# Two residual additions as identity products, and an order of its own for the first attention

## The chip, the cores and the metric

The kernel runs on one core of one Trainium2 chip. Times are microseconds (us) on the device for one launch. A core has five engines that run side by side, each with its own instruction queue: PE (TensorE, matrix products[...]), DVE (VectorE), ACT (ScalarE), POOL (GpSimd) and SP (which here only issues transfers). Each engine takes its instructions in the order in which they stand in its queue. The kernel before was timed three times: 9422.48, 9424.92 and 9425.63 us.

## What is computed

Two layers, each with a residual, on x of 8 images, 256 channels, 48 x 48 = 2304 positions. Layer 0 is an attention over positions that keeps the 16 most similar ones. Layer 1 is a stack of two selective scans (Mamba) over the 2304 positions.

```python
def _L0_conv_ref(x, W, bias):
    tokens = x.reshape(b, c, n).transpose(0, 2, 1)
    feat_pos = tokens @ W.T + bias
    feat, pos = feat_pos[:, :, :c], feat_pos[:, :, c:]
    pos = pos / jnp.maximum(norm, 1e-12)
    sim = jnp.einsum('bnc,bmc->bnm', pos, pos)
    topksim, topkid = jax.lax.top_k(sim, K)              # K = 16
    attn = jax.nn.softmax(topksim, axis=-1)
    out = jnp.einsum('bnk,bnkc->bnc', attn, topkfeat)
...
def step(h, inp):                                        # one of 2304 steps, 512 channels x 16 states
    dt_t, B_t, C_t, x_t = inp
    dA = jnp.exp(dt_t[:, :, None] * A)
    h = h * dA + dt_t[:, :, None] * B_t[:, None, :] * x_t[:, :, None]
    y = jnp.einsum('bds,bs->bd', h, C_t)
...
# --- layer 0 (conv_preact) ---
x = x + _L0_conv_ref(_gn(x), L0_conv_W, L0_conv_bias)
# --- layer 1 (conv_preact) ---
x = x + _L1_conv_ref(_gn(x), ...)                        # two Mamba layers, each after a layer norm
```

The change concerns the two lines `x = x + ...`.

## The kernel before

**The two parts of the program.** The attention of image 0 runs alone at the start (`layer0(..., alone=True)`, lines 591 to 617). After that the scans of images 0 to 7 run one after another, and beside the scans of image b the attention of image b + 1 is carried out, a little at each step (class `Ahead`). The last image has no attention beside it.

**Units and half steps.** An image's positions are cut into 6 chunks of 384. A *unit* is one chunk of one of the two Mamba layers, so there are 12 units an image and 96 in all, in an order in which the second layer runs two chunks behind the first. A unit has 16 *steps*. A step handles 32 of the 512 channels with all 16 states, laid out as 32 channels x 4 groups of states on the 128 partitions and 4 states along the free dimension. A step falls into two *half steps* of two states each. The main loop runs over half steps m; a unit has 32 of them.

**What a half step does.** POOL makes the forcing term of a whole step, `bx` (L907, 128x1536), two steps ahead. ACT makes the two decays of a half step (L928), one half step ahead, into one of two PSUM banks. DVE runs the scan (L943). The product of the states with C is then taken either by DVE (L945, for one half step, letter V in the string `SHARE`) or by POOL (L971, for one or both half steps of the step before, letter G). PE sums the states into `y` (L989), and with that frees the `bx` buffer, of which there are 8. `SHARE` has three strings of 32 letters: the first for the units 1 to 9 of an image, beside which the top-k of the next image runs, the second for the other units, the third for the last image.

**Tables.** All the other work of a unit (loads, layer norm, projections, taps, softplus, silu, gates, `out_proj`, `leave`) is placed by hand in tables of pairs (half step, function). Negative half steps lie in the unit before, those above 31 in the unit after. `between` and its kin come ahead of the half step's scan in the program, `behind` and its kin after it. The tables with `_spare` are for the units without top-k, those with `_last` for the last image.

**The attention.** Its 18 blocks of 128 positions take 16 half steps each, two blocks a unit. The list `within` says at which half step of its block each part stands: similarities on PE and their copies on ACT (`similar`, `keep_similar`, for blocks two ahead), the top-k on DVE (`top`, four instructions of 2.54 us), the turned weights (`turn`, `weights`), the weighted sum (`weigh`), then `average` (22), `turn_back` and `finish` (both 24). The same list serves for the attention of image 0, where no scan runs beside it and only the order of the instructions counts. Before its blocks each attention has a preparation of some 50 half steps (projections, norms), which starts at half step `EARLY` of the image ahead. The blocks begin at the next half step that fits into a raster of 16.

**The two residual additions.** `finish` (L551, DVE) adds the transposed attention in PSUM to the rows of x in SBUF. The rows come by a transfer that `average` issues on SP for every third block, into one of three buffers of the tag "x". `leave` (L1024, DVE) adds, for the second Mamba layer, the product in PSUM, a bias and the rows of x1 in SBUF, and a transfer takes the sum out. For the first Mamba layer `leave` is a copy on ACT (L1020). PSUM tiles of PE come from four banks used in turn (tag "mm"). A bank is free when its reader, here the DVE addition, is done.

Of the kernel before, what the change touches and what calls it, by code (L numbers as in the profile page):

```python
# [11 lines left out]
AF = mybir.ActivationFunctionType  # L12
ALU = mybir.AluOpType
# [3 lines left out]
P = 128  # L17
# [9 lines left out]
def tile_conv_preact(  # L27
# [18 lines left out]
    nc = tc.nc  # L46
# [5 lines left out]
    CB = C // P  # L52
    DB = DI // P
# [3 lines left out]
    TB = T // P  # L57
# [14 lines left out]
    FOLDED = (2, 3,)  # L72
    EARLY = -21


    SHARE = (
        "GGVGGGVGGGVVGVGGGGGVGGGVGGGGGVVG",
        "GVGGGVVVGGVVGGGGVGGVGGVVVGVVGVGV",
# [182 lines left out]
    def layer0(b, left, pool, ps0, alone):  # L261
# [229 lines left out]
        def invert(t):  # L491
            nc.vector.reciprocal(blocks[t]["den"], blocks[t]["den"])

        def others(t, i):
# [36 lines left out]
        def average(t):  # L531
            row = blocks[t]
            row["o"] = pool.tile([P, C], F32, tag="o", name=f"o_{b}_{t}", bufs=more)
            nc.scalar.activation(row["o"], row["po"], AF.Identity, scale=row["den"])
            if t % TB == 0:
                tag, bufs = ("xr", 2) if alone else ("x", 3)
                rows[t // TB] = load_chunk(pool, x[b], t // TB, tag, f"xr_{b}_{t}", bufs)

        def turn_back(t):
            row = blocks[t]  # L540
            row["pr"] = mm0(C, f"pr_{b}_{t}")
            for cb in range(CB):
                nc.tensor.transpose(
                    row["pr"][:, cb * P : (cb + 1) * P], row["o"][:, cb * P : (cb + 1) * P], ident
                )

        def finish(t):
            row = blocks[t]
            c, j = divmod(t, TB)
            xr = rows[c][:, :, j * P : (j + 1) * P]  # L550
            nc.vector.tensor_add(xr, xr, row["pr"].rearrange("p (k t) -> p k t", k=CB))  # L551
            if j + 1 == TB:
                xr = rows.pop(c)
                for cb in range(CB):
                    nc.vector.bn_stats(st1[:, cb, c, :], xr[:, cb, :])
                nc.sync.dma_start(x1[:, c * T : (c + 1) * T].rearrange("(k p) t -> p k t", p=P), xr)
            row.clear()
# [5 lines left out]
            (16, weigh, 0), (1, top, 1), (-9, similar, 0), (-7, similar, 1), (-7, similar, 2), (22, average),  # L563
            (-6, similar, 3), (-7, keep_similar, 1), (-3, keep_similar, 3), (-1, top, 0),
            (-3, keep_similar, 4), (15, turn, 1), (10, others, 4), (5, others, 0), (3, top, 2), (6, add_top),
            (12, invert), (5, others, 2), (17, turn, 2), (20, turn, 3), (24, finish), (15, weights, 1),
            (18, turn, 4), (18, weights, 2), (21, weigh, 3), (7, others, 1), (19, weights, 4), (21, weigh, 4),
        ]
        begin = min(part for part, *_ in within)
        parts = {}  # L570
# [433 lines left out]
    def out_proj(unit, cb):  # L1004
        pw = unit["pw"][cb] = mm(T, f"pw_{unit['u']}_{cb}")
        for k in range(DB):
            nc.tensor.matmul(  # L1007
                pw, unit["ow"][:, k, cb * P : (cb + 1) * P], unit["z"][k],
                start=(k == 0), stop=(k == DB - 1),
            )  # L1010

    def leave(unit, cb):
# [9 lines left out]
        else:  # L1022
            res = unit["res"]
            nc.vector.scalar_tensor_tensor(  # L1024
                res[:, cb, :], unit["pw"][cb], b_feat[:, cb : cb + 1], res[:, cb, :], ALU.add, ALU.add
            )
# [25 lines left out]
        (-3, load_rep, "dt", 1), (-29, load_in, 2), (5, in_proj, 7), (-20, tap, 0), (-15, taps, 1),  # L1052
        (-2, load_rep, "dtx", 3), (38, leave, 1), (22, load_rep, "dtx", 15), (-8, load_in, 4), (-37, mean),
        (-19, taps, 0), (5, load_d, 1), (-19, in_proj, 1), (-10, load_bc, 0), (-30, root_end),
        (-9, times_x, 0), (29, gate, 2),
    ]
    between_spare = [
        (25, sum_states, 2), (-34, variance), (-21, in_proj, 0), (38, out_proj, 0), (-15, taps, 2),
        (-35, square), (39, leave, 0), (23, load_rep, "dt", 14), (5, load_rep, "dt", 5),
# [8 lines left out]
        (7, load_rep, "dt", 6), (17, load_rep, "dt", 12), (-6, load_rep, "dtx", 1), (-14, load_in, 7),  # L1068
        (37, gate, 3), (-31, root), (9, load_rep, "dt", 7), (5, load_d, 1), (-24, load_in, 3),
        (17, load_rep, "dt", 11), (14, load_rep, "dtx", 11), (-13, x_proj), (-17, load_in, 6), (-3, load_d, 0),  # L1070
# [8 lines left out]
        (-2, load_rep, "dtx", 3), (8, copy_z, 1), (22, load_rep, "dtx", 15), (-16, load_in, 4), (-38, mean),  # L1079
        (-22, normal), (-37, center), (-21, in_proj, 1), (-12, load_bc, 0), (-30, root_end), (-9, times_x, 0),  # L1080
        (-25, load_in, 1), (-28, scale),
# [9 lines left out]
        (-17, tap, 1), (21, load_rep, "dt", 13), (-20, tap, 0), (-10, step_size, 1), (-5, load_rep, "dt", 0),  # L1091
        (9, copy_z, 2), (-18, in_proj, 2), (2, load_rep, "dtx", 5), (10, sum_states, 0),
        (13, load_rep, "dt", 9), (33, gate, 2), (-2, in_proj, 4), (9, silu_z), (7, load_rep, "dt", 6),
# [125 lines left out]
```

## Time and profile before

| what | value |
|---|---|
| median of three runs | 9424.92 us |
| the profiled execution, own time | 9422.82 us |
| its span in the profile | 9421.1 us |
| granted TensorE clock, mean | 0.898 |
| L551, the additions of the attention, DVE | 144 of 407 ns, 58.6 us |
| L1024, the additions of the scan part, DVE | 96 of 606 ns, 56.4 us |
| L907, forcing terms, POOL | 1536 of 3462 ns, 5307.1 us |
| L971, products with C, POOL | 1317 of 2455 ns, 3233.3 us |
| L943, scans, DVE | 3072 of about 1.75 us, 5327.1 us |
| L928, decays, ACT | 6144 of 585 ns, 3592.8 us |
| L378, copy 128x256 from PSUM, ACT | 144 of 364 ns |
| L792, Identity with bias, 128x384 from PSUM, ACT | 24 of 567 ns |

How to read it: a line of groups gives the busy time of one instruction of the source, how often it ran and the mean time of one. The recorded times of one engine overlap a little from one instruction to the next, so the distance between starts is some 0.1 us less than the duration (a scan that lasts 1.75 us is followed by the next one after 1.67). A line of waits names the engine and line that waited, what released it, the sum in us, how often, and the longest. In a timeline the columns are start, duration, engine, line, operation, and in brackets the idle time before it with what ended it. The first scan starts at 468 us; POOL and DVE are busy 8782 and 8598 of the 8953 us from there to the end.

### The profile page before, as it was taken

The page shows a single profiled execution, that of the slowest core. Times are in us where ns is not written, and L with a number is a line of the kernel's source. Part 1 is how long each engine was busy: PE and PEld are TensorE (multiplying, and loading weights), DVE is VectorE, ACT ScalarE, POOL GpSimd, SP SyncE. Part 2 cuts the span into 40 slices and gives each one's busy share as a digit, 9 for nine tenths or more (in the row PEclk, how much of TensorE's full clock was granted, in tenths as well). Part 3 has the DMA queues.
Part 4 walks back from the last instruction along what each step waited for, and adds up shares of the span by engine and source line. Part 5 has one row for each costly group of instructions (what it writes and reads, how often), then busy time and mean ns, then how long its engine had stood idle before and what let it go on. Part 6 is the DMA issues. An engine that isn't in the chain of part 4 may idle for free. (4 is left out here: it accounts for less than half of the span.)

```text
span 9421.1 us, 120485 instructions
## 1 busy us (share of the span) xinstructions
PE 7867.0 (84%) x37049; PEld 4423.6 (47%) x37049; DVE 8867.3 (94%) x7543; ACT 7307.1 (78%) x16242; POOL 8867.9 (94%) x3605
## 2 busy tenths in 40 slices
PE   8888987888878898798878988788887888877676
PEld 6644544455544554455444545445554455433332
DVE  6599999999989999899999999999999999989999
ACT  4578877788778877787878787778877788777776
POOL 2199999999999999999999999999999999999999
PEclk9989998899989998899988999889998899988877
DMA  4134444444444444444444434443444344444443
GB/s 128 50 123 136 134 137 152 129 136 137 136 151 129 133 140 131 151 131 139 131 144 138 140 128 140 145 138 127 138 134 157 122 141 132 138 153 145 149 147 126
DMA packets 1029829, 1275.91 MB, mean 135 GB/s; under 512 B 106529, under 2 KB 998945, under 8 KB 1028417
## 3 DMA queue, kind: packets, MB, share of 16 engines
q1 hardware_dynamic: 1028640, 1268.21, 42.0%
q8 instruction: 296, 4.85, 0.2%
q14 instruction: 349, 2.85, 0.1%
q10 hardware_dynamic: 544, 0.00, 0.0%
HBM read 1050.77 MB, written 217.06 MB: 135 GB/s over the span
## 5 line engine op out<-in xcount | busy, mean ns | idle before, releaser
L907 POOL TENSOR_TENSOR bx<-BC,dtxr 128x1536 f32<-128x1536 f32 x1536 | 5307.1, 3462 | 33.0 <-PE y L989 30.4
L928 ACT ACTIVATE da<-dtr,A_sb 128x385 f32<-128x385 f32 x6144 | 3592.8, 585 | 928.3 <-DVE bx L943 601.8
L943 DVE TENSOR_TENSOR_SCAN bx<-da,bx 128x770 f32<-128x770 f32 x1986 | 3423.7, 1746 | 85.1 <-ACT da L928 78.7
L971 POOL TENSOR_TENSOR bx<-bx,BC 128x1536 f32<-128x1536 f32 (+1 forms) x1317 | 3233.3, 2455 | 103.7 <-DVE bx L943 91.6
L943 DVE TENSOR_TENSOR_SCAN da<-da,bx 128x770 f32<-128x770 f32 x1086 | 1903.4, 1753 | 125.5 <-ACT da L928 123.1
L527 PE MATMUL po<-feat,aT 128*128 128x256 f32 x5184 | 1378.8, 415 | 236.6 <-ACT dt L842 107.3
L698 PE MATMUL pe<-vn,inw 128*128 128x384 f32 (+1 forms) x2976 | 1175.7, 524 | 216.0 <-ACT vn L775 100.6
L527 PEld LDWEIGHTS po<-feat,aT 128*128 128x128 f32 x5184 | 1022.0, 205 | 633.9 <-ACT aT L516 167.4
L456 PE MATMUL psim<-pos 128*128 128x512 f32 x2520 | 1203.2, 619 | 130.6 <-DVE xr L551 85.4
L989 PE MATMUL y<-bx,sel 128*32 128x384 f32 x12288 | 1221.6, 527 | 72.7 <-POOL bx L971 72.4
L945 DVE TENSOR_TENSOR bx<-da,BC 128x768 f32<-128x768 f32 x1086 | 1040.6, 958 | 37.4
L698 PEld LDWEIGHTS pe<-vn,inw 128*128 128x128 f32 x2976 | 567.6, 201 | 648.0 <-ACT vn L775 125.1
L456 PEld LDWEIGHTS psim<-pos 128*128 128x128 f32 x2520 | 504.4, 209 | 709.8 <-issue 385.3
L989 PEld LDWEIGHTS y<-bx,sel 128*32 128x32 f32 x12288 | 400.5, 117 | 866.6 <-issue 683.2
L803 DVE SCALAR_TENSOR_TENSOR xc<-pe,cw,xc 128x384 f32<-128x384 f32 x1080 | 655.4, 612 | 33.2 <-ACT xc L794 7.8
L516 ACT ACTIVATE aT<-pt 128x512 f32<-128x512 f32 (+1 forms) x720 | 387.7, 547 | 330.9 <-PE pt L508 328.6
L1007 PE MATMUL pw<-z,ow 128*128 128x384 f32 x1536 | 551.0, 505 | 57.5 <-ACT aT L516 38.5
L507 PE MATMUL pt<-ident,sim 128*128 128x128 f32 x2592 | 540.1, 289 | 13.4 <-DVE v L762 5.6
L986 PE MATMUL y<-xc,dmat 128*128 128x384 f32 x768 | 380.7, 581 | 157.7 <-DMA dmat<-diag 43.7
L499 ACT ACTIVATE rest<-left,three 128x512 bf16<-128x512 f32 (+1 forms) x720 | 453.5, 669 | 64.6 <-DVE left L484 64.6
L508 PE MATMUL pt<-minus,rest 128*128 128x128 bf16 x2592 | 496.1, 225 | 3.0 <-ACT rest L499 3.0
L959 ACT COPY h_st<-da 128x2 f32<-128x2 f32 x884 | 138.5, 157 | 419.9 <-DVE bx L945 409.2
(160 smaller groups left out, 9933.9 us busy)
## 6 DMA issues: line engine op xcount, KB each, us to landing
dtxr<-dtx_d SPq DMA_DIRECT2D x1536, 192.0 KB, 2.9
dtr<-dt_d SPq DMA_DIRECT2D x1536, 192.0 KB, 2.8
BC<-bc_d SPq DMA_DIRECT2D x192, 768.0 KB, 5.6
inw<-in_in_wT_dram SPq DMA_DIRECT2D x744, 128.0 KB, 2.5
dtx_d<-dtx SPq DMA_DIRECT2D x384, 192.0 KB, 1.9
dt_d<-dt SPq DMA_DIRECT2D x384, 192.0 KB, 2.0
ow<-in_out_wT_dram SPq DMA_DIRECT2D x96, 512.0 KB, 4.5
dmat<-diag SPq DMA_DIRECT2D x384, 64.0 KB, 2.7
```

Source lines behind the costliest of these rows:

```text
L456: nc.tensor.matmul(pm, pos[:, k, t * P : (t + 1) * P], pos[:, k, c0 : c0 + w], start=(k == 0), stop=(k == CB - 1),)
L507: nc.tensor.transpose(pt[:, q], row["sim"][:, r], ident)
L527: nc.tensor.matmul(row["po"], aT[:, m % PT, :], feat[:, m, :], start=(m == 0), stop=(m == NB - 1))
L698: nc.tensor.matmul(pe, w[:, k], unit["vn"][:, k, lo:], start=(k == 0), stop=(k == CB - 1))
L803: nc.vector.scalar_tensor_tensor(unit["xc"][e], unit["pe"][e][:, k : k + T], cw[:, unit["d"], e, k : k + 1], unit["xc"][e], ALU.mult, ALU.add,
L907: nc.gpsimd.tensor_tensor(bx[:, :, 1:], unit["BC"][0], unit["dtxr"][i].unsqueeze(1).to_broadcast([P, Q, T]), ALU.mult,)
L928: nc.scalar.activation(da[:, s * (1 + T) : (s + 1) * (1 + T)], unit["dtr"][i], AF.Exp, scale=A_sb[:, unit["d"], i, p * HQ + s : p * HQ + s ...
L943: nc.vector.tensor_tensor_scan(h, da, g, 0.0, ALU.mult, ALU.add)
L945: nc.vector.tensor_tensor(bx[:, :, 0:T], da.rearrange("p (q t) -> p q t", q=HQ)[:, :, 1:], unit["BC"][1][:, qs], ALU.mult,)
L971: nc.gpsimd.tensor_tensor(g[:, :, 0:T], g[:, :, 1:], unit["BC"][1][:, qs], ALU.mult)
L989: nc.tensor.matmul(y[j * G : (j + 1) * G, :], sel, unit["bx"][k * J + j][:, q, 0:T], start=False, stop=True, skip_group_check=True,)
L1007: nc.tensor.matmul(pw, unit["ow"][:, k, cb * P : (cb + 1) * P], unit["z"][k], start=(k == 0), stop=(k == DB - 1),)
```

## The change

1. `turn_back` gets, after each of its two transposes, a product of the identity with 128 columns of the rows of x, accumulated onto the same PSUM columns. `finish` becomes a copy from PSUM to SBUF on ACT.
2. `out_proj` gets, for the second Mamba layer, a fifth product, of the identity with the rows of x1, accumulated onto the same bank. `leave` becomes an Identity with bias on ACT.
3. The load of the rows of x moves from `average` (half step 22 of the block) to `invert` (12).
4. The first attention gets a list of its own, `first_order`. In `within` one entry moves by one half step.
5. The first string of `SHARE` has its letters at half steps 13 and 14 exchanged. The preparation of the next image starts at -24 instead of -21.
6. Five entries of the tables move: the load of the fourth dtx two half steps earlier (`behind`), `variance` two later and `root` one earlier (`between_spare`), `root_end` one earlier (`behind_spare`), and one `in_proj` three earlier (`between_last`).

```diff
-    EARLY = -21
+    EARLY = -24
...
-        "GGVGGGVGGGVVGVGGGGGVGGGVGGGGGVVG",
+        "GGVGGGVGGGVVGGVGGGGVGGGVGGGGGVVG",
...
         def invert(t):
             nc.vector.reciprocal(blocks[t]["den"], blocks[t]["den"])
+            if t % TB == 0:
+                tag, bufs = ("xr", 2) if alone else ("x", 3)
+                rows[t // TB] = load_chunk(pool, x[b], t // TB, tag, f"xr_{b}_{t}", bufs)
...
             nc.scalar.activation(row["o"], row["po"], AF.Identity, scale=row["den"])
-            if t % TB == 0:
-                tag, bufs = ("xr", 2) if alone else ("x", 3)
-                rows[t // TB] = load_chunk(pool, x[b], t // TB, tag, f"xr_{b}_{t}", bufs)
...
                 nc.tensor.transpose(
                     row["pr"][:, cb * P : (cb + 1) * P], row["o"][:, cb * P : (cb + 1) * P], ident
                 )
+                nc.tensor.matmul(
+                    row["pr"][:, cb * P : (cb + 1) * P], ident,
+                    rows[t // TB][:, cb, t % TB * P : (t % TB + 1) * P],
+                    start=False, stop=True, skip_group_check=True,
+                )
...
-            nc.vector.tensor_add(xr, xr, row["pr"].rearrange("p (k t) -> p k t", k=CB))
+            nc.scalar.copy(xr, row["pr"].rearrange("p (k t) -> p k t", k=CB))
...
-            (-6, similar, 3), (-7, keep_similar, 1), (-3, keep_similar, 3), (-1, top, 0),
+            (-5, similar, 3), (-7, keep_similar, 1), (-3, keep_similar, 3), (-1, top, 0),
...
+        first_order = [
+            (-9, similar, 0), (-9, similar, 2), (-8, keep_similar, 0), (-7, similar, 1), (-7, keep_similar, 1),
+            (-5, similar, 4), (-5, keep_similar, 2), (-3, similar, 3), (-3, keep_similar, 3),
+            (-3, keep_similar, 4), (-1, top, 0), (1, top, 1), (3, top, 2), (4, top, 3), (5, others, 0),
+            (5, others, 2), (6, others, 1), (6, add_top), (9, others, 3), (10, others, 4), (11, turn, 0),
+            (12, turn, 1), (12, invert), (13, turn, 3), (14, turn, 2), (15, weights, 1), (15, turn, 4),
+            (16, weights, 0), (16, weigh, 0), (18, weigh, 1), (18, weights, 2), (19, weights, 4),
+            (20, weigh, 2), (21, weights, 3), (21, weigh, 3), (21, weigh, 4), (23, average), (24, turn_back),
+            (24, finish),
+        ]
+        if alone:
+            within = first_order
...
-                start=(k == 0), stop=(k == DB - 1),
+                start=(k == 0), stop=(k == DB - 1 and "res" not in unit),
             )
+        if "res" in unit:
+            nc.tensor.matmul(pw, ident, unit["res"][:, cb, :], start=False, stop=True)
...
-            nc.vector.scalar_tensor_tensor(
-                res[:, cb, :], unit["pw"][cb], b_feat[:, cb : cb + 1], res[:, cb, :], ALU.add, ALU.add
+            nc.scalar.activation(
+                res[:, cb, :], unit["pw"][cb], AF.Identity, bias=b_feat[:, cb : cb + 1]
             )
...
-        (-2, load_rep, "dtx", 3), (38, leave, 1), (22, load_rep, "dtx", 15), (-8, load_in, 4), (-37, mean),
+        (-4, load_rep, "dtx", 3), (38, leave, 1), (22, load_rep, "dtx", 15), (-8, load_in, 4), (-37, mean),
...
-        (25, sum_states, 2), (-34, variance), (-21, in_proj, 0), (38, out_proj, 0), (-15, taps, 2),
+        (25, sum_states, 2), (-32, variance), (-21, in_proj, 0), (38, out_proj, 0), (-15, taps, 2),
...
-        (37, gate, 3), (-31, root), (9, load_rep, "dt", 7), (5, load_d, 1), (-24, load_in, 3),
+        (37, gate, 3), (-32, root), (9, load_rep, "dt", 7), (5, load_d, 1), (-24, load_in, 3),
...
-        (-22, normal), (-37, center), (-21, in_proj, 1), (-12, load_bc, 0), (-30, root_end), (-9, times_x, 0),
+        (-22, normal), (-37, center), (-21, in_proj, 1), (-12, load_bc, 0), (-31, root_end), (-9, times_x, 0),
...
-        (9, copy_z, 2), (-18, in_proj, 2), (2, load_rep, "dtx", 5), (10, sum_states, 0),
+        (9, copy_z, 2), (-21, in_proj, 2), (2, load_rep, "dtx", 5), (10, sum_states, 0),
```

## The prediction

> **What bounds the kernel now.** I read the page's busy line, the slices, a table of windows (one for each unit of 32 half steps of the fourth image), who waited for whom in nine of these units, and the timeline at one wait.
>
> ```profile
> PE 7867.0 (84%) x37049; PEld 4423.6 (47%) x37049; DVE 8867.3 (94%) x7543; ACT 7307.1 (78%) x16242; POOL 8867.9 (94%) x3605
> DVE  6599999999989999899999999999999999989999
> POOL 2199999999999999999999999999999999999999
> ```
>
> GpSimd and VectorE are busy for 94% each, and all of what they lack lies in the first two slices. So the 9421.1 us have two parts: about 468 us of first attention and start, and 8950 us in which both engines are nearly full.
>
> ```profile
> 4160.50:4255.10 94.60, 86.74 (x413) 49.22 (x413) 93.48 (x79) 77.21 (x176) 94.60 (x36) 0.93 0.42 135
> 4255.10:4352.00 96.90, 83.77 (x409) 47.22 (x408) 95.44 (x81) 78.56 (x177) 95.03 (x36) 0.95 0.43 139
> 4829.00:4918.60 89.60, 62.86 (x308) 32.55 (x308) 82.08 (x76) 67.09 (x154) 88.95 (x44) 0.82 0.46 149
> ```
>
> The columns are the window, its length, then the busy time of PE, weight loads, DVE, ACT and POOL. In the first window (an odd unit, with two blocks of the next image's attention) POOL has no idle time at all: 94.60 of 94.60. In the second (an even unit) POOL lacks 1.9 us and DVE 1.5 us. In the third (no top-k any more) DVE lacks 7.5 us and POOL 0.65. So the POOL work is the floor everywhere, and in the units with top-k DVE stands right beside it. What a lighter DVE can bring is what POOL waits, no more. These waits, over units 1 to 9 of that image:
>
> ```profile
> POOL bx L971 <- DVE bx L943: 6.3, 4, 2.2
> POOL bx L971 <- issue: 1.6, 1, 1.6
> POOL bx L907 <- PE y L989: 0.7, 1, 0.7
> ```
>
> 6.3 us in 4 waits for a DVE scan, one in each of four units. The timelines of POOL and of DVE show where one of them lies:
>
> ```profile
> 4297.10 1.74 POOL L971 TENSOR_TENSOR bx<-bx,BC 128x768 f32<-128x768 f32 x1
> 4298.75 3.49 POOL L907 TENSOR_TENSOR bx<-BC,dtxr 128x1536 f32<-128x1536 f32 x1
> 4304.10 3.17 POOL L971 TENSOR_TENSOR bx<-bx,BC 128x1536 f32<-128x1536 f32 x1 [1.87 <-DVE bx L943]
> ```
>
> ```profile
> 4299.18 1.75 DVE L943 TENSOR_TENSOR_SCAN bx<-da,bx 128x770 f32<-128x770 f32 x1
> 4300.85 0.40 DVE L551 TENSOR_TENSOR xr<-xr,pr 128x256 f32<-128x256 f32 x1
> 4301.28 1.02 DVE L555 BATCH_NORM_STATS2 st<-xr 128x6 f32<-128x384 f32 x2
> 4302.22 3.39 DVE L943 TENSOR_TENSOR_SCAN bx<-da,bx 128x770 f32<-128x770 f32 x2
> ```
>
> This is the middle of the unit, step 7. POOL has done a half product for step 6 (1.74) and a forcing product (3.49), and then waits 1.87 us for the scan of half step 15, which began at 4302.22. Ahead of it on DVE stands the addition of L551.
>
> **What the Trainium skill says.** "Perfetto Trace Analysis", section "Identifying the Most-Contended Engine": for Vector, Scalar and GPSIMD the occupancy is a fair measure, for matmul busy time it isn't. The trace agrees for the first three (94.60 of 94.60 is full). The same page, "Optimizing Scalar/DVE Operations": where DVE is saturated, moving an operation to ScalarE may pay. DVE is saturated in the top-k units, ACT is busy 77 to 79 of 95 us there. "SBUF — State Buffer", "Who interferes with whom": a DVE instruction with at most one SBUF input does not contend with GpSimd. Both removed additions have one input in PSUM and one in SBUF, so POOL's products should not get shorter by their removal. The trace agrees as far as it can: all 1536 products of L907 last 3413 to 3587 ns.
>
> **The change part by part.** The work on POOL doesn't change: both patterns for the top-k units have 23 G and 9 V.
>
> (a) *Additions taken from DVE.* 144 of L551 at 407 ns = 58.6 us and 96 of L1024 at 606 ns = 56.4 us, 115 us in all. 18 of the L551 lie in the first attention. In the middle units it is two L551 and one L1024 each, 2 x 0.41 + 0.61 = 1.4 us of about 95. The waits of DVE for these go as well (25.8 and 23.6 us over the trace). Since POOL is the floor, this counts only through POOL's waits for DVE.
>
> (b) *The pattern.* Half steps 12 to 15 go from G V G G to G G V G. At the place shown, POOL's part of step 6 becomes a whole product (3.17 instead of 1.74), and the part of step 7 becomes a half one. So POOL comes to its wait 1.43 us later, and the scan it waits for comes 0.43 us earlier (4300.85 to 4301.28, the addition that is gone). 1.43 + 0.43 = 1.86 against a wait of 1.87: the wait goes. Nothing is late next there, since DVE still does one V before that scan.  I take nine tenths of 6.3, which is 5.6 us an image, and there are seven images with such units: -39 us. Bounds: nothing if DVE keeps its lateness (then the wait moves one step on), and all of POOL's 8.6 us in these units, 7 x 8.6 = -60.
>
> (c) *Work put on ACT.* 144 copies of 128x256 from PSUM, nearest row L378 at 364 ns: 52 us. 96 Identity with a bias of 128x384, nearest row L792 at 567 ns: 54 us. ACT idles some 17 us in every middle unit, mostly waiting for DVE, so the 1.3 us of work hide. The new waits are those of an in-order engine for PE. For `finish` in the odd blocks of an image, ACT reaches its place in the trace about 4.3 us after `average` starts, and the transposes start at 4.4; transposes and identity products then take some 0.9. So ACT stands for about 1 us, behind it are the copy of the next similarities and the decays of the half step after the next, and DVE has a scan of 1.7 us before it needs those. In the even blocks the transposes are long done. For `leave` the ACT copies of the first depth do this already (78.9 us of waits in 42 cases, 1.9 each) and in the units with these DVE has no wait for ACT. Nothing, then, in the top-k units. In the first unit of an image it is different: the two `leave` come at half steps 6 to 8, the silu of z with its two table loads at 9, DVE waits for ACT at 9 to 13 (1.0 to 1.8 us each) and POOL for DVE at 14 (3.27 us in every image). Two activations of 0.57 that were not on ACT before go straight into that chain, 1.1 us, and some wait for PE: I take +1.5 an image, 7 x 1.5 = +10 us. Bounds: 0 (hidden behind an earlier wait) and 3 us an image (+21).
>
> (d) *Work put on PE.* In the trace a record of 256 columns repeats after 0.215 us at full clock, and a product has two records. The 288 identity products of 128 columns are then 0.22 each, 62 us, and the 96 of 384 columns 0.64 each, 62 us. That is 1.5 us for a middle unit, in which PE shows 8 to 13 us of idle. What it gains: the next similarities waited 154.4 and 85.4 us for the additions of L551, since these held a PSUM bank. I take nothing for both. Bound on the bad side below, as a rival.
>
> (e) *The first attention.* PE is the bound here: 93 to 95 busy of each 100 us between 100 and 400 us, ACT and DVE have a third or more free. PE's timeline at one block:
>
> ```profile
> 360.04 2.86 PE L527 MATMUL po<-feat,aT 128*128 128x256 f32 x12 [0.30 <-ACT aT L516]
> 363.50 0.44 PE L543 MATMUL pr<-ident,o 128*128 128x128 f32 x2 [0.60 <-ACT o L534]
> 363.78 1.47 PE L446 MATMUL psim<-ident,tri 128*128 128x128 f32 x12
> ```
>
> Each block loses 0.60 us before the transposes back, waiting for the scaling on ACT. The new order puts two similarity tiles between them, which at this block are eight transposes of 0.11 us: the wait goes. Added are two identity products, 0.43 us. Net -0.17 a block, 17 blocks: -3 us. Bounds: -12 if the 0.30 before the weighing goes too and the block's other small gaps with it, +8 if a new wait takes the place of the old one (18 x 0.43).
>
> (f) *Loads and small moves.* The load of the rows comes ten half steps earlier. Its buffers are three; by the tables each one is released at least four half steps before the new load asks for it, so SP doesn't stand, and the identity product finds its rows long there (3.8 us to land). The fourth dtx load moves ahead of the stores of the last dtx on SP. SP stands there for that POOL product anyway (180 us in 28 waits over seven units), and the buffer it needs is free when the first forcing product ends, before that. The preparation of the next image starts 3 half steps earlier, while its blocks start where they did, since they are aligned to 16: ACT and PE work moves from the first unit to the last one of the image before. These and the other moves in the tables I take at 0, bounds 2 us an image either way (14).
>
> (g) *The end.* The last product gets one identity product more, 0.64 at full clock, and the last addition is 0.57 on ACT instead of 0.62: +0.6.
>
> Sum: -39 + 10 - 3 + 0.6 = -31 us. The profiled execution took 9422.8 us (span 9421.1 and 1.7 around it), so 9392. The median of the runs is 9424.9, 2.1 above it: 9394 for the median.
>
> **Rivals.**
> 1. *DVE's relief reaches further.* In the first units and at the ends of images POOL lacks another 12 us an image, and 7 times some 22 us are all of POOL's gaps in the middle, about 160 us. If half of them go, 9424.9 - 80 = 9345. For it: 91.6 us of POOL's waits name DVE scans. Against: in the first units DVE waits for ACT, which gets more work.
> 2. *The wait only moves.* Bank, ACT and POOL hand the 1.9 us on to the next step: the gain of (b) is nothing, the cost of (c) stays, with the first attention and the end +8: 9424.9, within a few us of before, say 9425 to 9433. For it: POOL and DVE are both full. Against: DVE gets 1.4 us a unit lighter.
> 3. *PE comes late (slower).* POOL can write a new forcing product only when PE has summed the states out of its buffer; POOL waited for that 32 times, 30.4 us. PE is in order and gets 1.5 us a unit at full clock, 1.7 at the 0.9 granted, all of it ahead of such sums. If PE's backlog there exceeds POOL's slack, each of the 84 units of the seven images gets up to 1.2 us longer: +100, less the 31: 9494. It decides as soon as POOL waits for PE in the top-k units, where it now does for 0.7 us in nine units. Half of that would be 9444. Against: 8 us or more of idle PE in each of these units, and the waits for L551 that go.
>
> **How the numbers follow.** A measurement here can tell about 0.2%, 19 us: faster is below 9406, slower above 9444. The forecast has 0.50, with an own range of 9365 to 9412 (-60 in (b) with the good ends of (e), and half of (b) lost), so 0.44 of it faster and 0.06 the same. Rival 1 has 0.20, faster. Rival 2 has 0.12, of which 0.10 the same and 0.02 slower. Rival 3 has 0.18, slower. Together 0.64, 0.16 and 0.20. The range reaches from 9335 into rival 1 to 9455 into the milder half of rival 3.
>
> **What would show it.** Right: L551 and L1024 gone from DVE, POOL's waits for L943 down by 40 us, the even units as long as the odd ones (95 us), new waits of ACT for `pr` and `pw` without new waits of DVE for ACT in these units; blocks of the first attention 0.2 us shorter. Wrong: POOL waiting for PE's y in the middle of the image (rival 3), POOL's wait for L943 back at another half step (rival 2), or the first unit of each image changed by more than 3 us.

## The result, and the profile after

The changed kernel takes 9369.1 us (median of four runs, 9364.7 to 9369.7) against 9425.3 us for the kernel before on the same chip. The ratio is 0.9938 with a 95% interval of 0.9923 to 0.9954: 56 us less. The forecast for the median was 9394, 31 us less. The profiled execution took 9369.7 us, its span is 9367.3.

The busy line of the changed kernel:

```profile
PE 7974.4 (85%) x37817; PEld 4521.5 (48%) x37817; DVE 8771.5 (94%) x7303; ACT 7379.4 (79%) x16482; POOL 8867.6 (95%) x3605
```

POOL's work is what it was (8867.9 before), in the same 3605 instructions. DVE has lost 96 us of work and 240 instructions, PE has gained 107 us and ACT 72. So the 54 us that the span lost are idle time of POOL. Of POOL's waits over the whole run, those for ACT's inverse root rose by 37 us and those for PE's sums fell by 18. Those for DVE's scans changed most, here first before, then after:

```profile
POOL bx L971 <- DVE bx L943: 91.6, 64, 3.3
```

```profile
POOL bx L988 <- DVE bx L960: 35.4, 65, 1.9
```

The lost time can be placed by the starts of the scans in the two traces (the first scan, then each 32nd):

| stretch | before | after | difference |
|---|---|---|---|
| up to the first scan | 468.0 | 454.4 | -13.6 |
| images 0 to 6 | 7953.6 | 7909.8 | -43.8 |
| image 7 | 987.9 | 990.4 | +2.5 |
| after the last scan | 11.6 | 12.7 | +1.1 |

Within an image (mean of the images 1 to 6, as in all means of six below), unit 0 lost 2.2 us, the units 1 to 9 together 4.2, and the units 10 and 11 gained 0.4. The windows that answer to those of before (an odd unit, an even one, one without top-k; the columns are window, length, then busy PE, weight loads, DVE, ACT, POOL):

```profile
4124.90:4219.20 94.30, 84.97 (x411) 48.39 (x410) 92.87 (x76) 77.78 (x178) 94.06 (x36) 0.92 0.41 132
4219.20:4315.50 96.30, 87.41 (x430) 50.61 (x428) 93.97 (x79) 79.48 (x181) 95.13 (x36) 0.95 0.43 141
4789.50:4878.90 89.40, 67.08 (x316) 34.98 (x316) 80.51 (x72) 68.42 (x158) 88.75 (x45) 0.82 0.45 147
```

POOL lacks 0.24 us in the odd unit, 1.2 in the even one (1.9 before), and 0.65 in the last one, as before. POOL's waits over the units 1 to 9 of that image are now:

```profile
POOL bx L988 <- DVE bx L960: 2.0, 6, 0.5
POOL dtx L870 <- ACT dt L859: 0.2, 1, 0.2
POOL bx L988 <- ACT xc L811: 0.2, 1, 0.2
```

That is 2.4 us, where it was 8.6. The scan is L960 here and POOL's product with C is L988. POOL's timeline in the middle of the even unit, where it stood 1.87 us before:

```profile
4261.13 3.18 POOL L988 TENSOR_TENSOR bx<-bx,BC 128x1536 f32<-128x1536 f32 x1
4264.27 3.46 POOL L924 TENSOR_TENSOR bx<-BC,dtxr 128x1536 f32<-128x1536 f32 x1
4267.92 1.68 POOL L988 TENSOR_TENSOR bx<-bx,BC 128x768 f32<-128x768 f32 x1 [0.19 <-ACT xc L811]
```

The whole product stands first and the half one after it, as the pattern says, and 0.19 us of the wait is left. Read so far, this looks like step (b) of the forecast. The experiments show that it isn't.

Two things are new. The forecast counted on no new waits of DVE for ACT in the units with top-k, but DVE in the units 2 to 8 of that image now waits for ACT's decays, 7.8 us in 12 waits, where one wait of 0.3 us was before (over the seven images 6.1 to 7.8 us each, before at most 1.2):

```profile
DVE bx L960 <- ACT da L945: 5.3, 11, 1.0
DVE da L960 <- ACT da L945: 2.5, 1, 2.5
```

And in unit 0 of each image POOL stands for ACT's inverse root of the next image's norms (3.7 to 4.7 us in each of the seven), shown for the same image:

```profile
POOL nt_rn L176 <- ACT rn L168: 4.7, 1, 4.7
POOL bx L988 <- DVE bx L960: 1.9, 1, 1.9
POOL bx L924 <- PE y L1006: 0.5, 1, 0.5
```

In the kernel before the same unit had these lines, 8.4 us in all:

```profile
POOL bx L971 <- DVE bx L943: 5.4, 2, 3.3
POOL bx L907 <- PE y L989: 3.0, 2, 2.5
```

### The profile page after: what moved, and what is told of

It reads as the page before. It is cut to its first block, busy times and chain, and to the rows that moved or that the text cites. A ratio compares the mean times of both kernels' runs of the same rounds, so it can differ in the third digit from the quotient of the medians.

```text
span 9367.3 us, 121925 instructions
## 1 busy us (share of the span) xinstructions
PE 7974.4 (85%) x37817; PEld 4521.5 (48%) x37817; DVE 8771.5 (94%) x7303; ACT 7379.4 (79%) x16482; POOL 8867.6 (95%) x3605
## 5 line engine op out<-in xcount | busy, mean ns | idle before, releaser
L924 POOL TENSOR_TENSOR bx<-BC,dtxr 128x1536 f32<-128x1536 f32 x1536 | 5309.9, 3463 | 14.1 <-PE y L1006 12.5
L960 DVE TENSOR_TENSOR_SCAN bx<-da,bx 128x770 f32<-128x770 f32 x1986 | 3422.8, 1746 | 124.0 <-ACT da L945 94.7
L988 POOL TENSOR_TENSOR bx<-bx,BC 128x1536 f32<-128x1536 f32 (+1 forms) x1317 | 3234.5, 2456 | 36.3 <-DVE bx L960 35.4
L960 DVE TENSOR_TENSOR_SCAN da<-da,bx 128x770 f32<-128x770 f32 x1086 | 1904.2, 1753 | 171.1 <-ACT da L945 169.2
L1006 PE MATMUL y<-bx,sel 128*32 128x384 f32 x12288 | 1267.0, 528 | 101.2 <-POOL bx L988 100.6
L715 PE MATMUL pe<-vn,inw 128*128 128x384 f32 (+1 forms) x2976 | 1140.8, 510 | 154.9 <-ACT vn L792 51.9
L456 PE MATMUL psim<-pos 128*128 128x512 f32 x2520 | 1133.3, 594 | 66.0 <-ACT xr L556 25.9
L715 PEld LDWEIGHTS pe<-vn,inw 128*128 128x128 f32 x2976 | 544.3, 194 | 571.4 <-ACT vn L792 76.0
L850 PE MATMUL pd<-dbl,dtp_sb 16*128 16x384 f32 x768 | 366.1, 619 | 133.8 <-DVE z L1012 65.9
```

Source lines behind the costliest of these rows:

```text
L456: nc.tensor.matmul(pm, pos[:, k, t * P : (t + 1) * P], pos[:, k, c0 : c0 + w], start=(k == 0), stop=(k == CB - 1),)
L715: nc.tensor.matmul(pe, w[:, k], unit["vn"][:, k, lo:], start=(k == 0), stop=(k == CB - 1))
L924: nc.gpsimd.tensor_tensor(bx[:, :, 1:], unit["BC"][0], unit["dtxr"][i].unsqueeze(1).to_broadcast([P, Q, T]), ALU.mult,)
L960: nc.vector.tensor_tensor_scan(h, da, g, 0.0, ALU.mult, ALU.add)
L988: nc.gpsimd.tensor_tensor(g[:, :, 0:T], g[:, :, 1:], unit["BC"][1][:, qs], ALU.mult)
L1006: nc.tensor.matmul(y[j * G : (j + 1) * G, :], sel, unit["bx"][k * J + j][:, q, 0:T], start=False, stop=True, skip_group_check=True,)
```

## The experiments

The theory at this point was the forecast's: POOL is the floor, and the pattern and the lighter DVE together take its waits in the middle of the units away. The rivals were that DVE's instruction time is the bound, and that the gain comes from the parts that were taken at nothing (order, preparation, tables). Each run was timed beside the kernel before on its own chip, so the differences of the medians below are against that run of before (9423 to 9428 us). The ratio is not formed from the medians, so the two columns can differ by some us (0.9931 is 65 us).

| run | median us | ratio to before, 95% interval | difference us |
|---|---|---|---|
| after | 9369.1 | 0.9938 (0.9923 to 0.9954) | -56 |
| order alone | 9405.3 | 0.9978 (0.9970 to 0.9987) | -20 |
| pattern alone | 9415.1 | 0.9990 (0.9982 to 0.9998) | -10 |
| additions alone | 9421.8 | 0.9995 (0.9987 to 1.0003) | -3 |
| the second addition alone | 9420.1 | 0.9994 (0.9986 to 1.0002) | -8 |
| order and additions | 9393.4 | 0.9969 (0.9957 to 0.9980) | -30 |
| after without the additions | 9372.2 | 0.9947 (0.9934 to 0.9959) | -51 |
| after without the pattern | 9370.0 | 0.9944 (0.9931 to 0.9958) | -55 |
| after with EARLY = -21 | 9377.8 | 0.9948 (0.9936 to 0.9961) | -50 |
| after with the old tables | 9358.2 | 0.9931 (0.9918 to 0.9943) | -69 |
| after, zeros by ACT | 9367.8 | 0.9938 (0.9925 to 0.9952) | -60 |
| old tables, root later | 9353.8 | 0.9927 (0.9914 to 0.9941) | -70 |
| the same, two more V | 9365.0 | 0.9941 (0.9927 to 0.9955) | -58 |

Executions of one kernel spread over 2 to 16 us here, so differences of less than 5 us between two rows say nothing by themselves. Where a trace shows the place, the place is given. A trace is one execution: that of the additions alone lies 11 us below the median of its runs, that of order and additions 8 below, and that of the old tables 13 above.

**1. The order alone** (kernel before, plus `first_order`).

```diff
+        first_order = [
...
+        if alone:
+            within = first_order
```

> The kernel before with the own order of the first attention and nothing else. If the reason of step (e) holds (the wait of the transposes back for ACT goes, 0.60 us a block, and here without the 0.43 us of identity products), the first scan starts 10 to 14 us earlier than 468 us and the rest of the run is as long as before: -10 to -14 us. If the gain of the first attention came from the additions moved to ACT instead, the first scan stays at 468 within 3 us.

The first scan starts at 451.8 us instead of 468.0, and the images are as long as before: the sum over images 0 to 6 is 7952.8 against 7953.6. So the order is worth 16 us by the first scan and 20 by the medians, more than the upper end. The blocks say 20 too: from the first transposes back to the last it is 277.7 us here, and 297.6 to 298.6 in the kernel before and in the runs 2 and 7, which have the same code there. What lies between the last block and the first scan differs by up to 5 us from run to run (59.5 to 64.4 us in eight of them), so the first scan is the rougher measure. PE's timeline of the changed kernel at one block shows more than the forecast counted:

```profile
344.80 3.83 PE L530 MATMUL po<-feat,aT 128*128 128x256 f32 x17
348.46 1.04 PE L446 MATMUL psim<-ident,tri 128*128 128x128 f32 x8
349.34 0.27 PE L543 MATMUL pr<-ident,o 128*128 128x128 f32 x1
349.45 0.39 PE L546 MATMUL pr<-xr,ident 128*128 128x128 f32 x2
```

The eight transposes do stand between the weighing and the transposes back, and the 0.60 us are gone: over the 17 blocks PE idles 12.7 us ahead of the transposes back before, and 0.6 in this run. But the weighing also runs in fewer pieces, 21 instead of 72, and PE's idle time ahead of them falls from 5.9 us to 2.6, while 4.1 us ahead of the turning are new. The last five full blocks take 16.0 us each before, 15.2 with the order alone, and 15.5 in the changed kernel, with two identity products more in each.

**2. The pattern alone** (kernel before, plus the two letters).

```diff
-        "GGVGGGVGGGVVGVGGGGGVGGGVGGGGGVVG",
+        "GGVGGGVGGGVVGGVGGGGVGGGVGGGGGVVG",
```

> The kernel before with the two letters of the pattern exchanged and nothing else. If POOL's work is the floor and its wait for the scan of half step 15 is what can be saved, each of these waits loses up to 1.43 us: -20 to -35 us in all, and POOL's wait for DVE scans in units 1 to 9 of an image falls from 6.3 to below 2 us. If DVE's instruction time is the bound (the rival), the exchange does nothing, since DVE has as many V as before: within 5 us of before.

10 us, between the two expectations. POOL's waits over the units 1 to 9 of the same image:

```profile
POOL bx L971 <- DVE bx L943: 5.1, 7, 1.8
POOL bx L907 <- PE y L989: 1.6, 4, 0.5
POOL bx L971 <- issue: 1.3, 1, 1.3
```

5.1 instead of 6.3, in seven waits instead of four: the wait is cut in pieces and in part passed on. Over the units 2 to 9 of all seven images POOL waits for scans 32.5 us before, all of it for the scan of half step 15. With the pattern alone it is 15.5 us, of which 1.7 are left at half step 15 and 11.7 stand at half step 27.

**3. The additions alone** (kernel before, plus `turn_back`, `finish`, `out_proj`, `leave` and the earlier load).

```diff
-            nc.vector.tensor_add(xr, xr, row["pr"].rearrange("p (k t) -> p k t", k=CB))
+            nc.scalar.copy(xr, row["pr"].rearrange("p (k t) -> p k t", k=CB))
...
-            nc.vector.scalar_tensor_tensor(
-                res[:, cb, :], unit["pw"][cb], b_feat[:, cb : cb + 1], res[:, cb, :], ALU.add, ALU.add
+            nc.scalar.activation(
+                res[:, cb, :], unit["pw"][cb], AF.Identity, bias=b_feat[:, cb : cb + 1]
             )
```

> The kernel before with both additions as identity products and the earlier load of the rows, but with the old pattern, order, EARLY and tables. If POOL is the floor, only the 0.43 us of L551 ahead of each POOL wait and the 0.8 us waits at the other additions come in: -10 to -25 us after the first scan, and the first attention gets 0 to 8 us longer. If DVE's instruction time is the bound, 1.4 us come off each of 63 units: -75 to -90 us. If PE's extra 1.5 us a unit or ACT's waits eat it: 0 to +20 us.

The median is 3 us below before, the profiled execution, at 9410.7, is the shortest of its runs. In it the first scan starts at 476.2, 8.2 us later than before: the identity products on a PE that is full, 18 x 0.43 = 7.7 (by the blocks 7.5: 305.2 us against 297.7). After the first scan it is 20.6 us shorter than before, within the first expectation. The units 4, 6 and 8 get 1.9, 0.8 and 1.7 us shorter (mean of six images), POOL's idle there falls from 1.8, 1.7 and 0.9 to 0.4, 0.3 and 0.0, with the old pattern. POOL's waits for scans in the units 2 to 9 of the seven images fall from 32.5 to 6.4 us. The units 1 to 9 together are 855.7 us, where the kernel before has 859.8 and the kernel after 855.5. So in this execution the additions alone give all that the kernel after has gained in these units; whether it is as much in the others, which take 11 us more at the median, no trace shows. Unit 0 gets 0.9 longer, the last image 1.6, and the end 1.4. DVE's 75 to 90 us are out.

**4. After without the pattern.**

```diff
-        "GGVGGGVGGGVVGGVGGGGVGGGVGGGGGVVG",
+        "GGVGGGVGGGVVGVGGGGGVGGGVGGGGGVVG",
```

> The kernel after with the old pattern. If the pattern and the lighter DVE only work together (the wait of 1.87 us needs 1.43 from one and 0.43 from the other), this loses 20 to 35 us against after: 9390 to 9405. If the lighter DVE alone is enough, it is within 5 us of after (9369).

Within 1 us of after. POOL's waits over units 1 to 9 of the image are 2.9 us:

```profile
POOL bx L988 <- ACT xc L811: 1.5, 1, 1.5
POOL bx L988 <- DVE bx L960: 1.4, 3, 0.6
```

Over the units 2 to 9 of the seven images POOL waits for scans 6.7 us here and 11.2 in the kernel after, where 7.8 stand at half step 27. So beside the other parts the lighter DVE is enough without the pattern, and the theory that both are needed falls.

**5. EARLY = -21** in the kernel after.

> The kernel after with EARLY = -21 again, all else as after. The earlier runs leave some 3 us an image open that neither the additions nor the order nor the pattern gives: unit 0 is 97.4 us with the additions alone and 94.2 in the kernel after, unit 1 94.5 and 93.6. If the earlier preparation of the next image is what gives them, this is 20 to 28 us slower than after, and unit 0 is back at 97 us. If the moves in the tables give them, it is within 5 us of after.

8.7 us slower than after by the medians, 6 by the differences to before: less than expected, though the place is right. Unit 0 is back at 97.9 us (94.2 in the kernel after), and its waits of POOL are:

```profile
POOL bx L924 <- PE y L1006: 5.5, 2, 3.8
POOL bx L988 <- DVE bx L960: 5.2, 2, 3.3
```

The 3.3 us for a DVE scan are those of the kernel before (half step 14, after the silu of z). With EARLY = -24 they are 1.9, and the waits for the state sums are 0.5 instead of 5.5. In exchange comes the wait for the inverse root, 4.7. Units 2 and 3 take back 2 of the 3.7 us, the units 1 to 11 together 2.9.

**6. The old tables** in the kernel after (the five entries of the tables as before, EARLY = -24).

> The kernel after with the five entries of the tables where they were, EARLY = -24 kept. The counterpart of the run with EARLY = -21: 20 to 28 us slower if the tables (above all the dtx load that no longer stands behind the stores of the last dtx on SP) give the 3 us an image, within 5 us of after if EARLY does.

Neither: it is 11 us faster than after by the medians, 13 by the differences to before, though the two intervals overlap by more than half (and the one profiled execution took 9370.8, no less than the kernel after). In that execution unit 2 is 2.2 us shorter (95.6 instead of 97.8), units 0 and 1 1.4 longer together. The moves in the tables are of no use beside EARLY = -24, and by the medians a loss, whose cause this trace doesn't show.

**7. The second addition alone** (`out_proj` and `leave` only, on the kernel before).

> The kernel before with the second addition alone (out_proj and leave) as an identity product. If the relief of DVE works through what comes before POOL's wait in the middle of the unit, it is this addition (two of 0.61 us and 0.8 us of waiting at half step 6) that empties the waits of POOL in units 4, 6 and 8: they get 1 to 2 us shorter each, units 2, 3, 5, 7 stay, unit 0 gets 1 to 2 us longer, 10 to 20 us less in all. If it is the addition of L551, which stands right ahead of the scan POOL waits for, these units stay within 0.5 us.

8 us less by the medians, though the interval reaches past no gain at all, and the profiled execution took 9425.9. Its units 4, 6 and 8 get 0.8, 0.9 and 1.5 us shorter, unit 0 1.4 longer, unit 10 0.5, the last image 2.7, and units 2, 3 and 5 stay within 0.3. Those are the places expected, though not the 10 to 20 us. POOL's waits for scans in the units 2 to 9 of the seven images are halved, from 32.5 to 16.1 us. So the gain in the middle of a unit comes for the most part (3.2 of the 4.4 us in units 4, 6 and 8) from what leaves DVE at half step 6, nine half steps ahead of the scan that POOL waits for: two additions and the 0.8 us that DVE stood for PE there. The first addition alone was not run.

**8. The zeros by ACT.** In unit 2 of the kernel after one chain costs DVE 2.47 us. PE's timeline has its head:

```profile
4063.04 1.88 PE L715 MATMUL pe<-vn,inw 128*128 128x387 f32 x4 [2.52 <-POOL vn L788]
4064.72 4.17 PE L530 MATMUL po<-feat,aT 128*128 128x256 f32 x12
```

ACT's and DVE's timelines show who stands behind it:

```profile
4068.93 0.47 ACT L537 ACTIVATE o<-po,den 128x256 f32<-128x256 f32 x1 [3.29 <-PE po L530]
```

```profile
4070.80 1.77 DVE L960 TENSOR_TENSOR_SCAN da<-da,bx 128x770 f32<-128x770 f32 x1 [2.47 <-ACT da L945]
```

PE waits for three columns of zeros that POOL sets when it gets to them, the weighted sums behind it on PE are late, ACT waits for these in order, and the decays of DVE's next scan stand behind that. The edit takes the zeros off POOL:

```diff
+    zero = const.tile([P, CB, H], F32, tag="zero", name="zero")
+    nc.gpsimd.memset(zero, 0.0)
...
-            nc.gpsimd.memset(vn[:, :, 0:H], 0.0)
+            nc.scalar.copy(vn[:, :, 0:H], zero)
```

> The kernel after, with the three zero columns ahead of an image's first chunk copied by ACT from a constant instead of set by POOL. In the kernel after, PE waits 2.5 us in unit 2 for that memset, which stands in POOL's queue behind its products, ACT waits for PE at the scaling of the average (3.29 us), and DVE for ACT (2.47 us). If that chain is what makes unit 2 97.8 us long, unit 2 gets 1.5 to 2.5 us shorter, seven times: -10 to -17 us against after (9369). If POOL is the floor there anyway, the 2.5 us turn up as POOL's and nothing changes (within 4 us).

Unit 2 gets 2.7 us shorter as the chain says, but unit 0 gets 1.3 and unit 3 0.9 longer, and the time is within 1.4 us of after (4 by the differences). POOL was then busy in the whole of units 1, 2 and 3: 93.7, 95.1 and 95.7 us, which is the length of each. A wait of DVE beside a POOL that is full costs little: here the second expectation was nearer.

**9. Order and additions** (the kernel before with both, nothing else).

> The kernel before with the order of the first attention and both additions; pattern, EARLY and tables as before. If the parts simply add up, this is 9425 - 20 - 3 = 9402, and the missing 30 us to after (9369) belong to the earlier preparation, which takes a POOL wait of 3.3 us out of unit 0 and 2.5 us out of unit 1 only where DVE is lighter. If order and additions help each other, it is at 9380 or below.

30 us less than before, 9393. By adding up it would be 23 less, so the two help each other a little at best (the runs here spread from 9386 to 9401). In units 0 and 1 POOL still lacks 9.4 and 4.5 us, as in the kernel before.

**10. After without the additions.**

```diff
-            nc.scalar.copy(xr, row["pr"].rearrange("p (k t) -> p k t", k=CB))
+            nc.vector.tensor_add(xr, xr, row["pr"].rearrange("p (k t) -> p k t", k=CB))
```

(and the same for `leave`, with no identity products)

> The kernel after with both additions back on DVE (no identity products, L551 and L1024 as before); order, pattern, EARLY, tables and the earlier load as after. If the lighter DVE is what the rest rests on, this loses what the forecast gave to it, and units 4, 6 and 8 have POOL's waits again: 9395 to 9405. If order, EARLY and pattern do it alone, it is within 8 us of after (9369).

3 us slower than after, 5 by the differences. The places are those of run 3, the other way round: the first scan comes at 448.7 (5.7 earlier than in the kernel after), units 4, 6 and 8 are 1.4, 1.2 and 2.1 us longer, and the last image is 2.7 shorter. POOL's waits for the scans over units 1 to 9:

```profile
POOL bx L983 <- DVE bx L955: 4.0, 7, 1.0
```

So of the 56 us the additions, which the change is named for, bring some 3 to 5, because what they save in the units with top-k they cost elsewhere for the most part. By the two traces they save 23 us in the units 1 to 9 of the seven images, and cost 5.7 up to the first scan, 8.3 in the units 0, 10 and 11, 2.7 in the last image and 1.3 at the end.

**11. The root later** (kernel after with the old tables, and POOL's half of the preparation's last inverse norm one half step later).

```diff
         inverse_norm(NCH - 1)
         yield
+        if not alone:
+            yield
         inverse_norm_end(NCH - 1)
         yield
-        yield
+        if alone:
+            yield
```

> The kernel after with the old tables (9358) and POOL's half of the last inverse norm of the preparation one half step later. In the kernel after POOL stands 4.7 us at half step 21 of unit 0 for ACT's root, which itself stands behind a table load. If that wait is a loss of POOL, the bound, unit 0 gets 2 to 4 us shorter, seven times: 9330 to 9345. If what waits for POOL there (the spread on PE and the projections behind it) then comes late, it is no faster than 9358.

9353.8 us, 4 below the old tables alone and 15 below after by the medians, 0 and 13 by the differences to before. The first expectation is missed. The wait of 4.7 us is gone from unit 0, whose waits of POOL are now:

```profile
POOL dtx L873 <- DMA dtx_d<-dtx: 2.1, 1, 2.1
POOL bx L991 <- DVE bx L963: 1.9, 1, 1.9
POOL bx L927 <- PE y L1009: 0.3, 1, 0.3
```

Unit 0 is 1.5 us shorter than with the old tables alone (93.2), but POOL then lacks 3.7 us in unit 1 (0.3 there). So a third of the wait is gained in unit 0; that the whole run gets shorter by it isn't shown. It has the lowest median of this study: ratio 0.9927 (0.9914 to 0.9941) to before. Against after, the intervals of both overlap, and the runs do not (9353.0 to 9355.4, 9364.7 to 9369.7), though they were made on different occasions.

**12. Two more V** (run 11 with half step 8 as V in the second and third pattern).

```diff
-        "GVGGGVVVGGVVGGGGVGGVGGVVVGVVGVGV",
-        "VVGGVVGGGVVVGGVVGGGVGGVVGVGVGVVV",
+        "GVGGGVVVVGVVGGGGVGGVGGVVVGVVGVGV",
+        "VVGGVVGGVVVVGGVVGGGVGGVVGVGVGVVV",
```

> The kernel with the root later, and one more V (half step 8, just ahead of where DVE waits for ACT's silu) in the second and third pattern, so that POOL has a half product of 1.5 to 1.7 us less in each of the 3 units without top-k of an image and in each of the 12 units of the last one. If POOL is the floor in these units and DVE's 5 to 12 us of idle there can take it, the units 10 and 11 and those of the last image get 1 to 1.5 us shorter: -20 to -35 us against 9354, most of it shown by the last image (989.7 us down to 972 to 978). If the chain from ACT's silu over DVE to POOL sets these units, they stay within 0.3 us each and the time within 5 us of 9354.

11 us slower than run 11, against both expectations. The last image is 996.7 us instead of 989.7. POOL's waits in it, first in run 11, then here:

```profile
POOL bx L991 <- DVE bx L963: 9.7, 20, 0.9
```

```profile
POOL bx L991 <- DVE bx L963: 37.5, 23, 3.2
```

POOL has some 20 us less to do and waits 28 us more for DVE. DVE's waits for ACT stay (51 us here, 54 in run 11). So in the units without top-k POOL is not the floor alone, though it has 1 us of idle in 83. DVE with what it waits for ACT makes a second path of about the same length: of the 11.5 us more on it in that image (12 products of 0.96) 7.0 came through. The units 0, 10 and 11, which got one product more each, stay within 0.2 us of run 11.

## Why the prediction was right, and where its sum was not

Direction, range and the floor in the units with top-k hold. POOL's work is unchanged, and what the run lost is POOL's idle time. Of the signs that it named for being right, POOL's waits for scans fell by 56 us (40 forecast), the blocks of the first attention are 0.8 us shorter (0.2), and the even units are down at 94.7 to 95.7 us except unit 2 (97.8); the sign that DVE gets no new waits for ACT failed. One reading was wrong from the start: what POOL and DVE lack does not all lie in the first two slices. After the first scan POOL idles 171 us (8953 less 8782) and DVE 355. That 9369 lies within the range, near its lower end, is in part luck, since (b) has nearly the right size for a wrong reason. By the steps of the forecast:

- **(a), the work taken from DVE, counts only through POOL's waits.** Shown: the additions, 115 us by their mean times (DVE's busy time fell by 96, as recorded times overlap), bring 3 us by themselves (interval -12 to +3) and 3 to 5 in the kernel after, and no run comes near the 75 to 90 us of a DVE bound. POOL's products did not get shorter, as forecast: the forcing terms last 3463 ns in the mean, 3462 before. The rule that the forecast took for this from the Trainium skill, "SBUF — State Buffer", section "Who interferes with whom", holds there only outside what it calls DVE's 2-port perf modes, a condition that the forecast left out. And the 94.60 of 94.60, which it sets beside the rule on occupancy for three engines, shows this for POOL alone.
- **(b), -39 us in the units 1 to 9.** The size is nearly right, 4.2 us an image or -30 us in seven images. Its reason is wrong. The forecast set the pattern's 1.43 us and the 0.43 us of L551 against the wait of 1.87. Run 4 shows that the pattern isn't needed, run 2 that it passes two fifths of the wait on to other half steps, run 7 that most comes from the addition at half step 6. The step that failed is to look for the lateness of DVE right ahead of the wait, when DVE is full: what had left it nine half steps before counted as well.
- **(c), ACT in the top-k units at nothing, unit 0 at +1.5 an image.** With the additions alone unit 0 is 0.9 longer, with the second one alone 1.4: right. The prices were right too, 366 and 572 ns. That DVE would not wait for ACT in the units with top-k was wrong: in the units 2 to 8 it is 4.0 to 7.7 us an image with the additions alone, and 1.6 to 2.4 in run 10, which has all parts but the additions. It seems to cost little, since POOL is full beside it. The last image, where the forecast had nothing, gets 2.5 us longer.
- **(d), PE's identity products, at nothing.** Right in the units: POOL's waits for PE's sums are 27.2 us in 24 cases with the additions alone, 30.4 in 32 before. (In the kernel after they are 12.5 in 13, but without the additions 10.8, so that is not their doing.) Rival 3 has no trace in the runs.
- **(e), the first attention, -3 us.** A mis-sized term: -13.6 at the first scan, just past its bound of -12. By the blocks the order gains 20, where 10 was reckoned (0.60 a block): it also takes breaks ahead of and within the weighing, which the forecast had only in its bound. The identity products cost 7.5 with the old order, as reckoned, and 6 with the new one (284.1 us against 277.7 and 278.4).
- **(f), EARLY and the tables, at nothing, 14 us either way.** The other mis-sized term, and with it unit 0, which lost 2.6 us in the mean of seven images, 18 in all, where (c) had +10. Taken out of the kernel after, EARLY is worth 6 to 9 us. In the mean of seven images it takes 5.0 us of POOL's waits for scans and sums out of unit 0 and 2.6 out of unit 1, against 4.6 for the inverse root that are new. Unit 0 gets 3.7 us shorter by it (mean of six), of which 2.9 come back in the units behind. The tables give nothing or a loss beside it.
- **(g), +0.6 at the end:** 1.1.

Measured by the trace, the sum is -13.6 for the start, -18 for seven times unit 0, -29.5 for the units 1 to 9, +3.7 for the units 10 and 11, +2.5 and +1.1: -54. What stays open is how the gains of pattern, EARLY, tables and the one moved entry of `within`, which no run took alone, share the 26 us between order with additions (-30) and after (-56). Taken out of the kernel after one by one, pattern, EARLY and tables are worth 1, 6 to 9, and -11 to -13. But on top of order and additions, pattern and tables bring 20 us (run 5, -50), and pattern and EARLY 39 (run 6, -69). So EARLY and the tables seem to stand in for each other. The traces show one place: POOL's idle time in unit 1 is 4.5 us in run 9, 2.7 in run 5, 0.3 in run 6 and none in the kernel after. No run had EARLY or the tables alone.

## What to carry to other kernels

Where two engines are both full, find which waits the one with no slack has, and count what leaves the other one well ahead of the wait too, not only the instruction just ahead of it. A part of a change that moves no work (an order of instructions, the start of a background task) can be worth more than the part that gives the change its name, so it needs a sum of its own. And an engine with 1% of idle need not be the only bound: test it with a small amount of work moved away from it, before more is built on that.

## What the runs showed of the hardware that was not expected

PE loses time at the first record of each piece. In the first attention the weighing records (256 columns) repeat every 0.215 us (at a granted clock of 1.00 from 100 to 400 us), and almost only the distance from the first record of a piece to its second is longer, 0.27 to 0.32 us: in 71 of 72 pieces before (of 8 or 12 records) and in all 21 after (most of 36). So fewer and longer pieces lose less; why the first distance is longer is not shown. And executions of one program on one core differed by up to 16 us (9409.6 to 9423.6 in the run with the pattern alone, 9410.7 to 9427.1 with the additions alone), while others kept within 3 us (9353.0 to 9355.4), so a single profiled execution can lie 11 to 13 us from its median. In the runs with a wide spread the shorter executions show a slightly higher granted clock (0.905 at 9409.6 us, 0.899 at 9423.6 with the pattern alone); which of the two causes the other is not shown. The kernel after has 0.906 in the profiled execution, the one before 0.898.
